# An eight-expert layer's lists in a four-layer transformer: the work beside the pieces goes three steps at a time, the next block's gathers are issued sooner, a layer norm's product changes its engine, and masked keys are made a cycle ahead

## The chip, the cores and the metric

The kernel is one launch on one core of one Trainium2 chip. The metric is the device time of the launch in microseconds (us), lower is better. A core has five engines that run side by side, each through its own instructions in order: TensorE (PE, matrix products and transposes), VectorE (DVE), ScalarE (ACT), GpSimd (POOL) and SyncE (SP, which here only issues transfers). They wait for one another, and for transfers, by semaphores.

## The reference

Four layers run over 4096 tokens of 128 numbers, 16 sequences of 256. Each layer adds a gated attention and a gated feed-forward part, both behind a layer norm that is scaled and shifted per sequence. Cut to what matters here:

```python
def _layernorm(x, axis=-1, eps=1e-05):
    m = jnp.mean(x, axis=axis, keepdims=True)
    v = jnp.var(x, axis=axis, keepdims=True)
    return (x - m) / jnp.sqrt(v + eps)

# layer l
h = _layernorm(x) * (1 + ca) + sa
x = x + ga * attention(h)
h = _layernorm(x) * (1 + cb) + sb
x = x + gb * ffn(h)

# layer 1's ffn: an encoder block of its own
src = ln(src + attention(src), ln1_g, ln1_b)      # 16 heads of 8
gates = softmax(src @ gW + gb)
top2_scores, top2_idx = top_k(gates, 2)
w = (one_hot(top2_idx, 8) * top2_scores[..., None]).sum(1)
h = relu(einsum('nd,edf->enf', src, W1) + b1)
y = einsum('enf,efd->end', h, W2) + b2
out = ln(src + einsum('ne,end->nd', w, y), ln2_g, ln2_b)
```

So each token goes to the two of eight experts with the largest gates. Layer 2's attention has again 16 heads of 8, with rotary positions and a causal mask.

## The kernel before, in words

Activations stand in SBUF with the 128 features on partitions, in eight blocks of 512 tokens. The parts around the change follow one another in time like this.

**Attention in units** (`attend8`). Layer 1's feed-forward part begins with an attention, and layer 2 has one; both go through the same loop. A block holds two sequences, and each is a unit of eight cycles. In a cycle TensorE multiplies keys by queries twice: for the maxima of one unit (`ps_max`, from the masked keys `km` and `q`), reduced on VectorE (`m`, L1342), and for the exponentials of the unit before (`ps_exp`), taken on ScalarE (`E`, L1347). In layer 2 GpSimd masks `E` (L1350). `start_unit` makes a unit's `km` on GpSimd, two products (L1223); it stands at the top of the unit's first cycle. `prepare` makes a block's normed input and its queries and keys, in layer 2 with rotary sums on GpSimd (`q`, L1654); `finish` takes the result on. After each cycle, `advance` lets every generator in `self.later` go one step to its next `yield`. A generator is a piece of work beside: its steps are written out between the cycles of the loop, and so get their places in each engine's order.

**The norm** (`normed_steps`). The mean comes from a product on TensorE, the difference `ln_xc` from VectorE, square, logarithm and exponential (`ln_sq`) from ScalarE, and the last product `xc * sq` from GpSimd.

**The lists.** Beside layer 1's second attention, `gates` routes each block and `listed` writes its tokens into lists by expert in DRAM (`rows`), eight scatters a block from GpSimd (L818); there are two halves of four blocks, with lists of their own. Then the loop over 46 *pieces* of 256 listed rows follows, 23 to a half. A piece's rows and its expert's weights are read by SP (`fetch`), the rows are transposed on TensorE and copied by VectorE (`turn`, `l_x`), two layers of the expert follow (`hidden`, `out`), and ScalarE copies the result and writes it to DRAM (`done`). Reads are two pieces ahead, and one `advance` follows each piece. The half 2 lists of blocks 4 to 7 are still being written when the loop begins.

**The tails.** For each block `tail` gathers the 2 x 512 results from `done`, eight gathers from GpSimd (L1469), two in a step; waits four steps; sums the results with their weights on VectorE (`list_sums`); appends the next block's tail to `later`; and ends with a norm and an addition to `x` on GpSimd. `tail(0)` is appended when half 1's pieces are done. Two buffers of `list_rows` alternate between blocks, and `list_sums` has two as well. What the loop over pieces leaves goes on beside layer 2's attention, whose `prepare` for block b runs `advance` until b + 1 tails are done.

Where `self.strict` is set, instructions stay on their engine in the order of the program text; elsewhere, a scheduler places them. A program order that a line of the text changes is so an order of each engine.

Of the kernel before, what the change touches and what calls it, by code (L numbers as in the profile page):

```python
# [209 lines left out]
def bc(ap, shape):  # L210
    return ap.to_broadcast(shape)


class _InOrder:


    def __init__(self, kernel, engine):
        self.kernel, self.engine = kernel, engine
# [13 lines left out]
class _Kernel:  # L232
    def __init__(self, ctx, tc, t, out):
        self.ctx, self.tc, self.nc, self.t, self.out = ctx, tc, tc.nc, t, out
        self.turn = 0
        self.strict = self.strict_all = False
        self.later = []
        self.in_pieces, self.listed_halves, self.tailed, self.holds = False, 0, 0, {}
        self.tails_begun = self.halves_done = 0
        self.dve, self.act, self.gps = (_InOrder(self, e) for e in (tc.nc.vector, tc.nc.scalar, tc.nc.gpsimd))  # L240


# [120 lines left out]
    def normed_steps(self, src, out):  # L363

        n = src.shape[-1]
        ps = self.bank()[:, :n]
        self.mm(ps, self.c("mean"), src)
        xc = self.ln.tile([P, BLK], F32, tag="ln_xc", name="ln_xc")[:, :n]
        self.dve.tensor_sub(xc, src, ps)
        sq = self.ln.tile([P, BLK], F32, tag="ln_sq", name="ln_sq")[:, :n]  # L370
        self.act.activation(sq, xc, AF.Square)
        yield
        yield
        ps = self.bank()[:, :n]
        self.mm(ps, self.c("mean"), sq)
        self.act.activation(sq, ps, AF.Ln, bias=self.eps5)
        self.act.activation(sq, sq, AF.Exp, scale=-0.5)
        yield
        self.gps.tensor_mul(xc, xc, sq)
        out.append(xc)  # L380
        yield
        yield
# [793 lines left out]
    def attend8(self, nt, group, prepare, finish, scale, causal=False, masks=(None, None)):  # L1176
# [16 lines left out]
        per = len(first)  # L1193
        units = group * NBLK
# [5 lines left out]
        def step(g):  # L1200
            try:
                next(g)
                return True
            except StopIteration:
                return False

        def run(g):
            while step(g):
                pass
# [4 lines left out]
        def start_unit(u):  # L1214
            blk, i = divmod(u, group)
            if i == 0:
                run(ready.pop(blk))
                if blk + 1 < NBLK:
                    ready[blk + 1] = prepared(blk + 1)
            d = U[u]  # L1220
            km = d["km"] = self.att.tile([P, 2, 2, NQ], F32, tag="km", name="km")
            for i in range(2):
                nc.gpsimd.tensor_scalar(km[:, :, i, :], d["k"], half[:, i : i + 1], 0.0, ALU.mult, ALU.add)  # L1223
# [77 lines left out]
        for cycle in range(-lead, units * per):  # L1301
            mx, ex = cycle + lead, cycle
            mu, mt = divmod(mx, per)
            eu, et = divmod(ex, per)
            live_m, live_e = mu < units, ex >= 0
            if live_m and mt == 0:
                start_unit(mu)
            mms = []
            if live_m:
                cs, t, j0 = first[mt]  # L1310
                nk = (t + 1) * P if causal else NQ
                d = U[mu]
                Sm = self.ps_max.tile([P, 1024], F32, tag="max", name="ps_max").rearrange("p (j c i k) -> p j c i k", j=2, c=len(cs), i=2)
                if qmask is not None:
                    for j in range(2):
                        o = Sm[:, j, :, :, nk - P : nk].rearrange("p c i k -> p (c i) k")
                        self.mm(o, self.ident16, bc(qmask.unsqueeze(1), [P, 2 * len(cs), P]), skip_group_check=True)
                for c in range(len(cs)):
                    for j in range(2):
                        r = slice(32 * (j0 + j), 32 * (j0 + j) + 32)  # L1320
                        mms.append((c, Sm[:, j, c, :, :nk], d["q"][r, cs[c], t * P : (t + 1) * P], d["km"][r, cs[c], :, :nk], qmask is None and c == 0))
            if live_e:
                xcs, xt, xj0 = then[et]
                q0 = xt * P if causal else 0
                e = U[eu]
                Se = self.ps_exp.tile([P, 1024], F32, tag="exp", name="ps_exp").rearrange("p (j c i q) -> p j c i q", j=2, c=len(xcs), i=2)
                if kmask is not None:
                    for j in range(2):
                        o = Se[:, j].rearrange("p c i q -> p (c i) q")
                        self.mm(o, self.ident16, bc(kmask.unsqueeze(1), [P, 2 * len(xcs), P]), skip_group_check=True)  # L1330
                for c in range(len(xcs)):
                    for j in range(2):
                        r = slice(32 * (xj0 + j), 32 * (xj0 + j) + 32)
                        mms.append((c, Se[:, j, c, :, q0:], e["k"][r, xcs[c], xt * P : (xt + 1) * P], e["qm"][r, xcs[c], :, q0:], kmask is None and c == 0))
            for c, o, lhsT, rhs, fresh in sorted(mms, key=lambda x: x[0]):
                self.mm(o, lhsT, rhs, start=fresh, skip_group_check=True)
            if live_m:

                a = self.m8[mu % 2][:, t, 8:9]
                dims = [list(a.ap[0]), [32, 2], [2 * P, len(cs)], [P + 16, 2]]  # L1340
                o = bass.AP(tensor=a.tensor, offset=a.offset + 2 * P * cs[0] + 32 * j0, ap=dims)
                nc.vector.tensor_reduce(o, Sm[:, :, :, :, :nk], AX.X, ALU.max, negate=True)  # L1342
            if live_e:
                if xj0 == 0:
                    e["E"] = self.att.tile([P, 4, len(xcs), 2, NQ], F32, tag="E8", name="E8", bufs=3)
                E = e["E"][:, xj0 : xj0 + 2, :, :, q0:]
                nc.scalar.activation(E, Se[:, :, :, :, q0:], AF.Exp, scale=scale)  # L1347
                if causal:
                    D = e["E"][:, xj0 : xj0 + 2, :, :, q0 : q0 + P].rearrange("p j c i q -> p (j c i) q")
                    nc.gpsimd.affine_select(D, D, [[0, 4], [1, P]], ALU.is_ge, 0.0, base=0, channel_multiplier=-1)  # L1350
            for f in held:
                f()
            held = []
            if live_m and mt == per - 1:
                held.append(lambda u=mu: less_maxima(u))
            if live_e and et == 0:
                held.append(lambda u=eu: values(u))
            if live_e and xj0 == 2:
                held.append(lambda u=eu, x=et, E=e["E"]: weighted(u, x, E))
            sides = [g for g in sides if step(g)]  # L1360
            self.advance()
            for g in ready.values():
                step(g)
        for f in held:
            f()
        for g in sides:
# [6 lines left out]
    def layer1_ffn(self):  # L1373
# [12 lines left out]
        nc.vector.tensor_scalar(gg, m[:, 5, :], self.v("i1_ln2_g"), None, ALU.mult)  # L1386
        nc.vector.tensor_scalar(go, m[:, 5, :], self.v("i1_ln2_b"), None, ALU.mult)
        self.list_tables(keep)
        comb = self.comb1
        sums = self.w.tile([P, 4, BLK], F32, tag="m3", name="list_sums")  # L1390
        got = sums[:, 2:, :].rearrange("p a (b j d) -> p (a b) j d", j=2, d=P)
# [2 lines left out]
        with ExitStack() as ctx:  # L1394
# [65 lines left out]
            def tail(blk):  # L1460

                half, t0 = divmod(4 * blk, 16)
                w = self.two_w[half]
                g = self.list_rows[:, 2 * (blk % 2) : 2 * (blk % 2) + 2, :].rearrange("p a (u i d) -> p (a u) i d", i=2, d=P)
                wT, acc = self.h1[:8, :], sums[:, blk % 2, :]
                for t in range(4):
# [1 line left out]
                        of = bass.IndirectOffsetOnAxis(ap=self.origin[half][:, i, t0 + t : t0 + t + 1], axis=0)  # L1468
                        nc.gpsimd.indirect_dma_start(g[:, t, i], None, self.done[half][:, :], of)  # L1469
                    yield  # L1470
                for _ in range(4):
                    yield
                ps = self.bank()
                for t in range(4):
# [6 lines left out]
                for i in range(2):  # L1481
# [3 lines left out]
                            acc[:, v], g[:, t, i], w[:, i, t0 + t : t0 + t + 1], acc[:, v] if i else ps[:, v], ALU.mult, ALU.add  # L1485
                        )
                    yield

                self.tails_begun = blk + 1
                if blk + 1 < 4 * self.halves_done:  # L1490
                    self.later.append(tail(blk + 1))
                y = self.sums_turned(acc)
                yield True
                xb = xf[:, blk * BLK : (blk + 1) * BLK]
# [66 lines left out]
            for n in range(-2, N + 2):  # L1561
                if n + 2 < N:
                    fetch(n + 2)
                if 0 <= n < N:
                    turn(n)
                if 0 <= n - 1 < N:
                    hidden(n - 1)
                if n >= 2:
                    out(n - 2)
                if n == NPIECE + 1:  # L1570
                    self.halves_done = 1
                    self.later.append(tail(0))
                self.advance()
            self.settle()
            self.halves_done = 2
            if self.tails_begun == 4:
                self.later.append(tail(4))
# [20 lines left out]
    def layer2_attn(self):  # L1598
# [5 lines left out]
        with ExitStack() as ctx:  # L1604
# [26 lines left out]
                yield  # L1631

            self.attend8(2, 2, prepare, finish, 1.0 / 11.3125, True, (below, None))

    def turned8(self, w, hb, out):

# [483 lines left out]
```

## Time and profile before

| | |
|---|---|
| time, median of three runs | 3413.59 us (3412.11, 3413.59, 3422.58) |
| the profiled execution | 3419.26 us, of which the span below is 3417.6 |
| PE busy | 3065.4 us, 90% |
| DVE busy | 1961.0 us, 57% |
| ACT busy | 1741.0 us, 51% |
| POOL busy | 1319.5 us, 39% |
| layer 1's second attention | 1770 to 2262 us |
| pieces of half 1, hole, pieces of half 2 | 2262 to 2316, to 2342.5, to 2398.7 us |
| layer 2's attention, up to its first maxima | 2398.7 to 2421.5 us |
| its units 0 to 7, and 8 to 15 | to 2694.8, to 2921 us |

A profile's times are microseconds from the span's start. "Busy" is the time in which an engine ran instructions. A row of the page names line, engine, operation, the tile written and those read, the number of instructions, busy time, mean duration in ns, and idle time of the engine before them with what ended it. L224 is the line of a helper through which VectorE, ScalarE and GpSimd operations go, L266 that of matrix products and L269 that of transposes, so rows are told apart by their tiles. PEclk is the clock that TensorE was granted, as a share of full speed.

### The profile page before, as it was taken

The numbers are of one execution on the slowest core, as the hardware profiler recorded it, in microseconds if no ns is written. First come the engines' busy times: TensorE is split into PE (matmuls) and PEld (weight loads), VectorE is DVE, ScalarE is ACT, GpSimd is POOL, SyncE is SP. The second block draws the span as 40 slices with busy tenths as digits, with TensorE's granted clock in tenths as the row PEclk, the third lists the DMA queues.
The fourth block names the chain that finished last, engine by engine and source line by source line (L and its number), as shares of the span: only waits on it lengthen the run. The fifth ranks groups of instructions, "written<-read, shape, count | busy, mean of one in ns | idle before, by whom it ended". The sixth has DMA issues, their size and how long they took to land. (4 is left out here: it accounts for less than half of the span.)

```text
span 3417.6 us, 51618 instructions
## 1 busy us (share of the span) xinstructions
PE 3065.4 (90%) x19100; PEld 1802.8 (53%) x19100; DVE 1961.0 (57%) x4563; ACT 1741.0 (51%) x4474; POOL 1319.5 (39%) x1167
## 2 busy tenths in 40 slices
PE   6999999979999999999987888886778899899887
PEld 3666666655666677766752333356334444455443
DVE  4777777744444566666654655531345575545564
ACT  3777777754222566666643544444124334575543
POOL 4777777730000233443430122124444343233355
PEclk9999999999999999999987999988789899999998
DMA  3030000000000600000000000036000000000000
GB/s 126 15 37 1 1 1 1 1 25 1 1 1 1 236 1 1 1 1 1 1 1 1 1 12 8 26 117 193 19 13 7 19 1 1 1 1 1 1 13 13
DMA packets 43179, 77.13 MB, mean 23 GB/s; under 512 B 5920, under 2 KB 22736, under 8 KB 42288
## 3 DMA queue, kind: packets, MB, share of 16 engines
q1 hardware_dynamic: 31888, 58.48, 5.8%
q0 software_dynamic: 4416, 9.33, 0.9%
q10 hardware_dynamic: 6624, 6.03, 0.5%
q8 instruction: 151, 2.47, 0.3%
q14 instruction: 100, 0.82, 0.1%
HBM read 44.69 MB, written 33.32 MB: 23 GB/s over the span
## 5 line engine op out<-in xcount | busy, mean ns | idle before, releaser
L224 POOL TENSOR_TENSOR E<-E,sm_inv 128x1024 f32<-128x1024 f32 (+1 forms) x256 | 430.1, 1680 | 480.6 <-PE ps_big L266 189.2
L1342 DVE TENSOR_REDUCE m<-ps_max 128x4 f32<-128x1024 f32 (+1 forms) x256 | 279.3, 1091 | 269.6 <-PE ps_exp L266 178.2
L1347 ACT ACTIVATE E<-ps_exp 128x1024 f32<-128x1024 f32 (+1 forms) x256 | 234.4, 915 | 370.0 <-PE ps_exp L266 289.6
L266 PE MATMUL ps_big<-h,w_f_W 128*128 128x512 f32 x768 | 361.1, 606 | 3.9 <-DVE s L981 3.9
L266 PE MATMUL ps_max<-km,q 32*128 32x512 f32 (+1 forms) x1024 | 296.9, 659 | 74.1 <-DVE m L1342 52.4
L224 ACT ACTIVATE E<-E,sm_neg 128x256 f32<-128x256 f32 x512 | 254.2, 497 | 198.6 <-DVE sm_neg L1071 198.6
L266 PE MATMUL ps_exp<-qm,q 32*128 32x512 f32 (+1 forms) x1024 | 287.6, 640 | 4.4 <-ACT E L1347 4.0
L269 PEld LDWEIGHTS ps_one<-w_cst,E 128*128 128x128 f32 x1792 | 203.6, 141 | 162.6 <-POOL E L224 109.6
L269 PE MATMUL ps_one<-w_cst,E 128*128 128x128 f32 x1792 | 243.3, 276 | 38.6 <-POOL E L224 38.4
L224 DVE COPY PT<-ps_one 128x512 f32<-128x512 f32 x320 | 208.8, 686 | 102.5 <-PE ps_one L269 101.6
L266 PE MATMUL ps_big<-kT,qT 64*128 64x256 f32 (+1 forms) x2048 | 264.9, 377 | 0.0
L266 PEld LDWEIGHTS ps_out<-w_f_W,s 128*128 128x128 f32 (+1 forms) x2048 | 188.6, 190 | 91.3 <-issue 40.4
L266 PE MATMUL ps_one<-PT,v 128*64 128x256 f32 (+1 forms) x2048 | 226.4, 364 | 1.4 <-DVE PT L224 1.0
L224 ACT ACTIVATE E<-ps_big,sm_neg 128x128 f32<-128x128 f32 (+1 forms) x512 | 208.8, 422 | 23.8 <-DVE sm_inv L224 22.0
L1071 DVE CUSTOM_DVE_ANT_0 E<-ps_big,bias 128x256 f32<-128x256 f32 x512 | 186.7, 421 | 48.6 <-PE ps_big L266 37.6
L266 PEld LDWEIGHTS ps_big<-h,w_f_W 128*128 128x128 f32 x768 | 137.7, 191 | 142.2 <-issue 119.9
L224 POOL TENSOR_TENSOR ln_xc<-ln_xc,ln_sq 128x512 f32<-128x512 f32 (+1 forms) x81 | 101.8, 1257 | 283.7 <-ACT ln_sq L224 228.3
L224 POOL TENSOR_TENSOR r_r<-r_r,r_t 128x512 f32<-128x512 f32 x128 | 162.5, 1270 | 124.9 <-DVE r_t L224 112.6
L266 PE MATMUL ps_out<-w_f_W,s 128*128 128x128 f32 (+1 forms) x2048 | 201.0, 281 | 10.4 <-DVE s L1744 10.1
L980 ACT ACTIVATE s<-ps_big,w_vecs 128x512 f32<-128x512 f32 x128 | 87.7, 687 | 222.6 <-PE ps_big L266 222.5
L266 PEld LDWEIGHTS ps_big<-kT,qT 64*128 64x128 f32 x2048 | 166.4, 187 | 58.1 <-issue 49.5
L981 DVE SCALAR_TENSOR_TENSOR s<-ps_big,w_vecs,s 128x512 f32<-128x512 f32 x128 | 95.9, 750 | 167.5 <-ACT s L980 167.5
(318 smaller groups left out, 6092.1 us busy)
## 6 DMA issues: line engine op xcount, KB each, us to landing
rows<-zeros SPq DMA_DIRECT2D x8, 2048.0 KB, 18.5
list_w<-in_f_W SPq DMA_DIRECT2D x46, 257.0 KB, 3.4
list_sums<-rows SPq DMA_DIRECT2D x46, 128.0 KB, 3.2
done<-l_o ACTq DMA_DIRECT2D x46, 128.0 KB, 3.4
rb_rows<-rb_d SPq DMA_DIRECT2D x1, 4088.0 KB
w_a_qkv<-in_a_qkv SPq DMA_DIRECT2D x2, 1536.0 KB
w_f_W<-in_f_W SPq DMA_DIRECT2D x3, 1024.0 KB
bias<-rb_rows SPq DMA_DIRECT2D x16, 192.0 KB, 4.3
```

The source lines that it names most:

```text
L224: ins = f(*args, **kw)
L266: self.ordered(self.nc.tensor.matmul(out, lhsT, rhs, start=start, stop=stop, **kw))
L269: self.ordered(self.nc.tensor.transpose(out, in_, self.c("ident")))
L980: nc.scalar.activation(s, gv[:, :BLK], AF.Silu, bias=self.v("b1_0", c))
L981: nc.vector.scalar_tensor_tensor(s, gv[:, BLK:], self.v("b2_0", c), s, ALU.add, ALU.mult)
L1071: nc.vector.tensor_tensor_reduce(e[:, i], S[:, i], bias[g][:, i, off : off + T], 1.0, BIG, ALU.add, ALU.min, neg[:, i : i + 1])
L1342: nc.vector.tensor_reduce(o, Sm[:, :, :, :, :nk], AX.X, ALU.max, negate=True)
L1347: nc.scalar.activation(E, Se[:, :, :, :, q0:], AF.Exp, scale=scale)
```

## The change

Four edits. The last product of a norm goes to VectorE while `lists_on` is set, which is from the start of layer 1's feed-forward part to the end of layer 2's attention. `start_unit` goes from the top of a unit's first cycle to the end of the cycle before. A tail appends its successor as soon as its own gathers are issued, waits until the tail two before it has summed (its buffer is then free), and between gathers and sums waits nine steps in the loop over pieces, four elsewhere. The loop over pieces calls `advance` three times after each piece.

```diff
     def normed_steps(self, src, out):
...
         yield
-        self.gps.tensor_mul(xc, xc, sq)
+        (self.dve if self.lists_on else self.gps).tensor_mul(xc, xc, sq)
         out.append(xc)
...
             live_m, live_e = mu < units, ex >= 0
-            if live_m and mt == 0:
-                start_unit(mu)
+            if mx == 0:
+                start_unit(0)
             mms = []
...
             for g in ready.values():
                 step(g)
+
+            if live_m and mt == per - 1 and mu + 1 < units:
+                start_unit(mu + 1)
...
         self.list_tables(keep)
+        self.lists_on = True
...
             def tail(blk):

                 half, t0 = divmod(4 * blk, 16)
+                while self.summed < blk - 1:
+                    yield
...
                         nc.gpsimd.indirect_dma_start(g[:, t, i], None, self.done[half][:, :], of)
                     yield
-                for _ in range(4):
+
+                self.tails_begun = blk + 1
+                if blk + 1 < 4 * self.halves_done:
+                    self.later.append(tail(blk + 1))
+                for _ in range(9 if self.in_pieces else 4):
                     yield
...
                     yield
-
-                self.tails_begun = blk + 1
-                if blk + 1 < 4 * self.halves_done:
-                    self.later.append(tail(blk + 1))
+                self.summed = blk + 1
                 y = self.sums_turned(acc)
...
-                self.advance()
+                for _ in range(3):
+                    self.advance()
             self.settle()
+            self.in_pieces = False
             self.halves_done = 2
...
             self.attend8(2, 2, prepare, finish, 1.0 / 11.3125, True, (below, None))
+        self.lists_on = False
```

More of the change, by code (lines that the diff above doesn't have):

```diff
@@ L238, in __init__ @@
         self.in_pieces, self.listed_halves, self.tailed, self.holds = False, 0, 0, {}
-        self.tails_begun = self.halves_done = 0
+        self.tails_begun = self.halves_done = self.summed = 0
+        self.lists_on = False
         self.dve, self.act, self.gps = (_InOrder(self, e) for e in (tc.nc.vector, tc.nc.scalar, tc.nc.gpsimd))
@@ L1633, in layer2_attn @@
             self.attend8(2, 2, prepare, finish, 1.0 / 11.3125, True, (below, None))
+        self.lists_on = False
     def turned8(self, w, hb, out):
```

## The prediction

> **What bounds the kernel now.** I read the page's slices first (a slice is 85 us; digits are tenths busy):
>
> ```profile
> PE   6999999979999999999987888886778899899887
> ...
> DVE  4777777744444566666654655531345575545564
> ...
> POOL 4777777730000233443430122124444343233355
> PEclk9999999999999999999987999988789899999998
> DMA  3030000000000600000000000036000000000000
> ```
>
> TensorE is at 9 tenths except around slices 21 to 31, which hold layer 1's second attention, its lists and layer 2's attention, the stretch that the change touches. The answer by windows splits it:
>
> ```profile
> core 0: us, PE busy (x) PEld busy (x) DVE busy (x) ACT busy (x) POOL busy (x), PEclk, DMA share, GB/s
> ...
> 1770.00:2262.00 492.00, 404.89 (x2694) 161.25 (x2692) 245.90 (x413) 215.18 (x302) 87.04 (x102) 0.88 0.03 10
> 2262.00:2316.00 54.00, 51.23 (x338) 47.93 (x338) 20.76 (x80) 27.28 (x68) 18.21 (x27) 0.92 0.69 206
> 2316.00:2342.50 26.50, 0.03 (x1) 0.06 (x1) 0.00 (x0) 0.22 (x1) 8.70 (x9) 0.54 0.12 37
> 2342.50:2398.70 56.20, 55.90 (x379) 51.16 (x379) 16.36 (x44) 31.77 (x77) 29.00 (x30) 0.97 0.82 244
> 2398.70:2421.50 22.80, 12.79 (x28) 4.25 (x27) 7.07 (x11) 3.60 (x5) 12.84 (x14) 0.83 0.09 26
> 2421.50:2694.80 273.30, 230.03 (x1412) 102.33 (x1416) 142.66 (x245) 83.90 (x135) 119.81 (x138) 0.83 0.05 14
> ```
>
> In order: second attention; pieces of half 1 (one piece is a transpose, two layers of an expert and a write, 1.98 us on PE); a hole of 26.5 us in which only POOL works; pieces of half 2, PE full; layer 2's start; its first four blocks. The chain of waits through the middle:
>
> ```profile
> 2333.04 2.23 DMA rows<-list_rows,l_i
> ...
> 2340.31 2.02 DMA list_sums<-rows
> 2343.13 1.71 PE ps_hid L266 x4
> ...
> 2399.15 1.74 DMA done<-l_o
> ...
> 2405.33 1.27 POOL ln_xc L224
> ...
> 2417.70 1.27 POOL q L1654
> ...
> 2420.47 1.02 PE ps_max L266 x4
> ```
>
> The hole is the list's scatters, each waiting for the one before, 2.50 us apart when quiet. Then PE sets the end up to 2398.7; then latency does, until the first scores. Finally, the lines of the gathers (the 32 before 2420) and of the norm's tile in the second attention:
>
> ```profile
> L1469 POOL DMA_INDIRECT list_rows<-done,origin x32: 947/952/1002, 2351.7 to 2403.0; - x32
> ...
> DMA to landing us min/median/max: 2.5/4.1/4.8
> ```
>
> ```profile
> L224 POOL TENSOR_TENSOR ln_xc<-ln_xc,ln_sq x16: 1255/1270/1282, 1779.2 to 2260.2; 128x512 f32<-128x512 f32 x16
> ...
> L224 DVE TENSOR_TENSOR ln_xc<-x,ps_one x8: 686/687/690, 1775.1 to 2111.7; 128x512 f32<-128x512 f32 x8
> ```
>
> A gather holds POOL 0.95 us; back to back, starts are 1.256 us apart. Under the pieces' DMA load they land after 3.3 to 4.8 us, else after 2.5.
>
> **What the Trainium skill says.** "VectorE: DVE Perf Modes", section on the TRN2 errata: an fp32 tensor_tensor takes (N+151)/0.96, 691 ns at N=512; the 687 above agrees. "GPSIMD Engine Reference", 3.1: the same work is 1.96 times slower there; here 1270/687 = 1.85. "DMA: Bandwidth & Descriptors", Anatomy of one DMA, SWDGE path: about 2.0 us and bytes/436e3, so 2.15 for 64 KB; measured 2.5 quiet, almost twice that loaded. "TensorE: Matmul & The Clock Gate", What's actually happening: an idle window of 3.4 us halves the clock; the 0.54 in the hole agrees.
>
> **The change part by part.** The built programs, compared engine by engine, give the orders below; the number of gathers (64), scatters (64) and pieces (46) is unchanged.
>
> *Masked keys.* No instruction changes place on any engine: end of one cycle and top of the next adjoin. 0.
>
> *Norm's product.* 39 products go from POOL to DVE, 0.58 us shorter each. DVE is half busy there, so they hide; uncovered they would cost 39 x 0.69 = 27 us. In the second attention four products stand behind scatters, which makes DVE wait 2.6 to 3.6 us before them; on DVE their consumers come 1.9 to 2.9 us sooner. Sum 10 us; the other twelve give 0.2 to 0.5 each or the reverse, since max-reduces queue behind them. Between 2 and 10, I take **-6**. In layer 2 22 products shorten by 0.6 a chain of which a part sets the end: 2 to 8, I take **-5**. A POOL stall moves rather than ends: the keys' products (km, L1223) still stand behind eight scatters twice (5 us each).
>
> *Three steps per piece, half 1.* The scatters remain 64, in one chain; neither SP's order of issues nor their number changes. PE waits for the last of half 2 as before; VectorE's wait for block 5's scatters grows from 5 to about 10 us inside the hole. 0 to -2, I take **-0.6**.
>
> *Half 2.* Now tails 0 to 3 are gathered and summed in it (before: all of tail 0, part of 1), and their DVE sums stand at fixed places among the copies x24 to x46 that feed the pieces: tail 0's behind x29, tail 1's x31, tail 2's x35, tail 3's x36. The first gather still waits for the last `done` write of half 1, 2351.7. 32 back to back: the last issues at 2351.7 + 31 x 1.256 = 2390.6 and lands 3 to 4.5 us later, 2393.6 to 2395. Before, x37 was ready near 2372. Behind x36, DVE waits for that landing; nine pieces queue behind x37: 2395 + 9 x 1.98 + about 3 us of tails' PE work = 2416 against 2394.6: **+21.5**. Bounds: +12 if the gathers land early and PE catches up, +25 if the load stretches their 1.256. What is late next is the whole of layer 2.
>
> *Layer 2's start.* Sixteen gathers (tails 4 and 5) now stand on POOL ahead of layer 2's first four q sums (L1654) and four km, and they wait for the last `done` of half 2, 2.8 us after the last piece. 16 x 1.256 = 20.1 us: the q sums begin 23 us after the last piece instead of 12.4, first scores at about 31 instead of 22.8: **+8** (+3 if the gathers begin before the last write lands, +11).
>
> *Layer 2's first eight units.* Before, tails 1 to 7 were done in them, with one hole of 14.1 us in unit 0 for tail 1, and gathers in bursts of eight, in which km or the causal mask's select (E, L1350) came 1.4 to 6.1 us late. Now tails 4 to 7 fall in units 0 to 3, and units 4 to 7 have none. Blocks without tails took 54.1, 56.1 and 50.5 us for two units. Units 4 to 7: 124.8 to 107, -18. Units 0 to 3, 148.3: the hole less 2, so -12, and three forced tails fewer against four bunched tails, -3. Sum **-33**, bounds -20 (bunched gathers hold the selects) and -50 (units 0 to 3 near 54 per block, and the clock, 0.50 there in the first 40 us, higher).
>
> Sum: -6 - 0.6 + 21.5 + 8 - 33 - 5 = -15 us. The profiled execution had a span of 3417.6 us and took 3419.3; the median of the runs is 3413.6, 5.7 lower. 3413.6 - 15 = about **3399 us**.
>
> **Rivals.**
>
> *POOL's queue becomes the bound (slower).* Place: from the first gather of half 2 to unit 3. The +29.5 of pieces and start is paid in full; then the last eleven gathers and tails 6 and 7 stand among the selects of units 0 to 3, so these give nothing, and the units give only -18; products give -1 instead of -11. +29.5 - 18 - 1 = +10.5, 3424. With the products at -1 the kernel is slower once units 0 to 7 take more than 245 us, by over 0.3% above 255. For it: POOL's share there is 44%, and its gathers held selects before. Against: fewer tails are left.
>
> *Even.* Half 2 and start at +30, units at -25, products at -5: 0, 3410 to 3415. For it: both sides are sums of waits that I sized to a third.
>
> *More gain.* Half 2 at +14, start +5, units -50, products -9: -40, 3374. For it: PE is idle 43 us in those units and its clock is 0.83 against 0.94 later, so what removes holes also restores clock. Against: the loss comes first and is near certain.
>
> *The change does nothing.* True of the masked keys, excluded for the rest, whose instructions move on PE, DVE, ACT and POOL.
>
> **How the numbers follow.** What a measurement here can tell from no change is 0.3%, 10.2 us. Chances: my sum, -10 to -30, 0.40; more gain 0.20; even, -10 to +10, 0.25; slower 0.15. So faster 0.60, same 0.25, slower 0.15. Of the rival with more gain I include half and of the slower nearly all: 3374 to 3426. The likeliest case alone is 3384 to 3404.
>
> **What would show it.** Right: unchanged orders' chain to 2342; TensorE waiting inside half 2 between 2365 and 2395, its releaser a copy x behind list_sums; the last piece near 2410; 16 gathers in a row ahead of the first q; first max-reduce near 2445; units 0 to 7 in 235 to 245 us with the 14 us hole gone; no gathers after unit 3. Wrong: no hole inside half 2, so that the sums wait for nothing (then a gain of 30 or more); units 4 to 7 still at 30 us each (then clock, not tails, set them, and the result is even or slower); a second attention longer than 492 us, with DVE's products in front of its max-reduces.

## The result, and the profile after

The changed kernel took 3406.09 us at the median of 15 runs (3398.76 to 3416.51), the kernel before 3415.35 in the same comparison (3406.17 to 3429.49). The ratio is 0.9965, 95% interval 0.9951 to 0.9979: 0.35% faster, which is the 12 us between the two means; the medians differ by 9.3. The forecast was 3399 us and -15.

The profiled execution of the changed kernel happens to be the slowest of its fifteen, at the lowest clock (0.946, up to 0.952 in the others): it took 10.4 us more than its median, the profiled execution of the kernel before 3.9 more. So the two profiles differ by 2.8 us only, and stages are read one by one. The slices of the page after:

```profile
PE   5999999979999999999987888886789989899887
...
DVE  4777777744444566666654656532356675545564
...
POOL 4777777730000233443430021124343333234355
PEclk9999999999999999999997999977789999999998
DMA  3030000000000600000000000044200000000000
```

The DMA's two full slices (3 and 6) have become 4, 4 and 2: the pieces' transfers are spread over a longer time. GpSimd's busy time fell by 48 us to 1271.3, VectorE's rose by 23 to 1984.0. By windows, with the same columns as before (busy us and instructions of the engines, clock, DMA share, GB/s):

```profile
core 0: us, PE busy (x) PEld busy (x) DVE busy (x) ACT busy (x) POOL busy (x), PEclk, DMA share, GB/s
1770.00:2257.70 487.70, 398.43 (x2709) 160.64 (x2705) 256.58 (x432) 215.44 (x302) 67.61 (x90) 0.89 0.04 11
2257.70:2312.40 54.70, 50.67 (x329) 47.33 (x329) 18.41 (x76) 27.24 (x68) 16.40 (x23) 0.88 0.68 203
2312.40:2339.00 26.60, 0.00 (x0) 0.00 (x0) 0.00 (x0) 0.35 (x1) 8.66 (x9) 0.56 0.11 33
2339.00:2419.50 80.50, 72.21 (x423) 60.62 (x424) 29.43 (x75) 38.31 (x89) 36.08 (x36) 0.89 0.62 176
2419.50:2451.70 32.20, 14.28 (x27) 4.67 (x25) 7.83 (x12) 3.59 (x5) 22.95 (x24) 0.69 0.15 41
2451.70:2690.20 238.50, 208.78 (x1356) 92.74 (x1356) 138.76 (x230) 76.07 (x123) 86.46 (x107) 0.87 0.04 12
```

The hole is as long as before. Half 2 went from 56.2 to 80.5 us, layer 2's start from 22.8 to 32.2, its first eight units from 273.3 to 238.5. Measured between marks that both traces share (the first maxima of an attention or a unit on VectorE, the first and last copies of rows in a half), and put beside the forecast:

| stage | before | after | difference | forecast |
|---|---|---|---|---|
| second attention, to the first piece's copy | 473.7 | 469.1 | -4.5 | -6 |
| half 1 and the hole | 77.9 | 78.8 | +0.9 | -0.6 |
| half 2, first copy to last | 51.5 | 75.3 | +23.8 | +21.5 |
| last copy to layer 2's first maxima | 26.9 | 36.7 | +9.8 | +8 |
| units 0 to 7 | 273.3 | 238.4 | -34.8 | -33, and most of -5 |
| units 8 to 15 | 200.7 | 200.7 | 0.0 | the rest of -5 |
| what follows | 518.8 | 520.6 | +1.8 | 0 |

The rows add up to -3 us, as the profiles do. The three stages of the lists (half 2, start, units 0 to 7) come to -1.2 together, the attention to -4.5. Where the rest of the 12 us lies, no stage of these two executions shows.

The start is seen in the chain of waits after. 16 gathers stand on GpSimd ahead of the first q sum; these are the last of them:

```profile
2427.64 6.71 PE ps_one L267 x10
2434.38 0.70 DVE q L1664
2435.32 0.96 POOL list_rows L1476
...
2441.61 0.95 POOL list_rows L1476
2442.58 1.28 POOL q L1665
2443.89 0.76 DVE rot_t L1662
...
2449.07 1.37 POOL km L1224 x2
2450.48 1.22 PE ps_max L267 x4
```

VectorE has its part of q ready at 2435; the sum begins at 2442.58. In half 2, VectorE's waits after are these:

```profile
engine line waited for: us in total, times, longest us
...
DVE list_sums L224 <- PE ps_one L267: 6.8, 4, 3.9
DVE list_sums L224 <- DMA list_rows<-done,origin: 5.3, 5, 1.6
DVE ln_xc L224 <- POOL x L224: 4.0, 1, 4.0
```

Only 5.3 us are waits for a gather to land, which the prediction made the cause of half 2's growth, and all of them fall into the sums of tails 0 and 1, before 2372. The times agree all the same: the 32nd gather was issued at 2389.3 and landed at 2393.0, copy x37 followed at 2394.7 and x46 at 2415.0. Between copies x36 (2387.3) and x37 VectorE ran tail 2's difference, tail 3's sums and the copy; the brackets hold its idle time before each, and what ended it:

```profile
2391.64 0.69 DVE L224 TENSOR_TENSOR ln_xc<-list_sums,ps_one 128x512 f32<-128x512 f32 x1 [3.97 <-POOL x L224]
2392.66 1.12 DVE L224 SCALAR_TENSOR_TENSOR list_sums<-list_rows,list_room,ps_one 128x128 f32<-128x128 f32 x4 [0.33 <-PE ps_one L267]
...
2394.75 0.42 DVE L1540 COPY l_x<-ps_in 128x256 f32<-128x256 f32 x1
```

It waited 4.0 us for GpSimd's addition of tail 0, which stands behind all 32 gathers, and for no gather. TensorE's waits in half 2, apart from the one that ends the hole:

```profile
PE ps_one L270 <- DVE list_sums L224: 6.0, 4, 2.4
PE ps_one L267 <- ACT h L224: 1.0, 1, 1.0
```

### The profile page after: what moved, and what is told of

Same layout as the page of the kernel before. It is cut to its first block, busy times and chain, and to the rows that moved or that the text cites. A ratio compares the mean times of both kernels' runs of the same rounds, so it can differ in the third digit from the quotient of the medians.

```text
span 3414.8 us, 51574 instructions
## 1 busy us (share of the span) xinstructions
PE 3058.7 (90%) x19100; PEld 1804.4 (53%) x19100; DVE 1984.0 (58%) x4602; ACT 1740.6 (51%) x4474; POOL 1271.3 (37%) x1128
## 4 chain that ended last, share of the span: by engine, by line
PE 61%; DVE 10%; ACT 4%; POOL 4%; DMA 3%; issue 3%; POOLq 0%; DVEq 0%; SPq 0%; ACTq 0%
PE ps_one L267 21%; PE ps_big L267 14%; PE ps_out L267 9%; PE ps_max L267 7%; PE ps_one L270 7%; DVE m L1343 4%; DMA rows<-list_rows,l_i 2%; PE ps_exp L267 2%; POOL E L224 1%; ACT ln_sq L224 1%; DVE ln_xc L224 1%; PE ps_hid L267 1%; DVE pv L224 1%; ACT E L1348 1%; POOL list_rows L1476 1%
## 5 line engine op out<-in xcount | busy, mean ns | idle before, releaser
L267 PE MATMUL ps_max<-km,q 32*128 32x512 f32 (+1 forms) x1024 | 289.1, 643 | 79.6 <-DVE m L1343 59.0
L267 PE MATMUL ps_exp<-qm,q 32*128 32x512 f32 (+1 forms) x1024 | 280.2, 625 | 4.4 <-ACT E L1348 4.0
L224 ACT ACTIVATE E<-ps_big,sm_neg 128x128 f32<-128x128 f32 (+1 forms) x512 | 208.8, 422 | 23.8 <-DVE sm_inv L224 21.8
L267 PEld LDWEIGHTS ps_max<-km,q 32*128 32x128 f32 x1024 | 84.0, 199 | 199.4 <-DVE m L1343 98.9
```

The costliest lines, as they stand in the source:

```text
L224: ins = f(*args, **kw)
L267: self.ordered(self.nc.tensor.matmul(out, lhsT, rhs, start=start, stop=stop, **kw))
```

## The experiments

These runs come from three chips: e1 to e4 from one, e5 to e8 from a second, e9 to e12 from a third. On them the kernel before took 3451 to 3457 us at the median instead of 3415, so they are compared with each other only, by ratios to the kernel before beside them on the same chip. Stage times of different chips are compared with some care: e4 and e6, one kernel on two of them, agree within 3 us in each stage. Stage times (us) are from one profile each, between the marks of the table above; "e" numbers are the order of the runs.

| kernel | attention | half 2 | start | units 0-7 | units 8-15 | ratio to before, 95% |
|---|---|---|---|---|---|---|
| e1 masked keys alone | 481.2 | 77.2 | 33.3 | 274.6 | 200.8 | 1.0002 (0.9984 to 1.0020) |
| e2 norm alone | 466.1 | 77.4 | 32.9 | 259.9 | 194.0 | 0.9914 (0.9886 to 0.9942) |
| e3 all but the norm | 483.4 | 97.9 | 36.2 | 238.5 | 201.7 | 0.9987 (0.9967 to 1.0006) |
| e5 the changed kernel | 465.8 | 98.4 | 36.6 | 237.3 | 200.7 | 0.9936 (0.9912 to 0.9961) |
| e4, e6 sums later | 466.5, 469.1 | 81.3, 81.5 | 27.1, 27.2 | 236.5, 236.5 | 194.7, 194.2 | 0.9872 (0.9843 to 0.9902), 0.9845 (0.9820 to 0.9870) |
| e7 gathers in text order | 466.0 | 98.1 | 28.6 | 232.0 | 200.7 | 0.9885 (0.9859 to 0.9910) |
| e8 one step per piece | 463.2 | 77.7 | 34.0 | 257.2 | 197.9 | 0.9910 (0.9885 to 0.9936) |
| e9 no tail in half 2 | 466.5 | 45.8 | 71.9 | 259.2 | 194.8 | 0.9939 (0.9915 to 0.9963) |
| e10 addition on VectorE | 466.3 | 97.0 | 36.7 | 237.0 | 200.7 | 0.9938 (0.9918 to 0.9958) |
| e11 norm and three steps | 466.3 | 108.2 | 36.7 | 234.3 | 200.5 | 0.9949 (0.9931 to 0.9966) |
| e12 e6 and e7 together | 469.5 | 82.9 | 26.6 | 234.5 | 200.7 | 0.9836 (0.9809 to 0.9862) |

### Masked keys alone (e1)

```diff
-            if live_m and mt == 0:
-                start_unit(mu)
+            if mx == 0:
+                start_unit(0)
...
+            if live_m and mt == per - 1 and mu + 1 < units:
+                start_unit(mu + 1)
```

> The kernel before with the masked keys' edit alone. My theory: no engine's order changes, so the time is that of before, ratio 1.000 within 0.2%, and every stage of the profile stands within 1 us of before's where the clock is the same. Rival: making km earlier removes its waits; then the units of both attentions would shorten by 3 us or more in all.

The ratio is 1.0002: this edit does nothing that shows within 0.2%. Its stages serve as those of the kernel before from here on. They were not within 1 us of the profile that was predicted from, which I had expected of them: half 2 took 77.2 us instead of 51.5, with the same instructions. That is taken up under e9.

### The norm's product, alone and left out (e2, e3)

```diff
-        self.gps.tensor_mul(xc, xc, sq)
+        (self.dve if self.lists_on else self.gps).tensor_mul(xc, xc, sq)
```

> The kernel before with the norm's product on VectorE alone. My theory: -6 us between the first and last max-reduce of layer 1's second attention (422.9 to 417), pieces and hole unchanged, and -5 in layer 2's first eight units (273.3 to 268): ratio 0.997. Rival 1, the lists carry the whole gain: 0 to -2, ratio 1.000. Rival 2, the norm is the whole gain and the lists' edits are worth nothing net: ratio 0.9965, units near 265.

> The changed kernel with the norm's product back on GpSimd. My theory: the second attention as before (423 us); pieces of half 2 longer than the changed kernel's 75 us from first to last copy of rows, since the tails' products then queue behind 32 gathers and VectorE's copies behind them: 80 to 90; start +9, units near 240: ratio 1.000 to 1.004. Rival, the lists carry the gain by themselves: half 2 as in the changed kernel or shorter, ratio 0.998 or less.

Norm alone gave 0.86%, far more than forecast: -15.1 us in the attention, -14.7 in units 0 to 7, -6.8 in the units after. The other edits alone gave 0.13%, within their interval of nothing. In the changed kernel the norm's worth is e3 to e5: -17.6 us in the attention, -1.2 in units 0 to 7, -1.0 after. So in units 0 to 7 the product and the lists' edits take away the same time, and only one of them is paid. (The -6.8 after them can't be put down to the product: see e12.)

That is rival 2 of e2, in sense if not in number: beside the norm, the lists' edits were worth nothing. Half 2, start and units 0 to 7 take 370.2 us together with the norm alone, 372.3 in the changed kernel (e5), and the ratios are 0.9914 and 0.9936. Half 2 did not suffer from products on GpSimd (97.9 against 98.4): I had expected 80 to 90 against 75, 5 to 15 more.

Why the attention is shorter was a surprise too. First the windows over it of e1, then of the changed kernel e5:

```profile
1790.50:2271.60 481.10, 398.39 (x2678) 160.22 (x2678) 247.15 (x411) 210.12 (x294) 81.77 (x91) 0.87 0.04 11
```

```profile
1790.70:2256.50 465.80, 382.50 (x2686) 156.70 (x2686) 254.83 (x434) 210.59 (x296) 63.41 (x81) 0.91 0.04 11
```

TensorE's idle time is the window less its busy time: 82.7 us and 83.3. It did not fall. Nearly the same products took 15.9 us less, at a granted clock of 0.91 instead of 0.87. On e1's own chip e2 shows the same: 13.5 us less busy at 0.90, with 81.1 us idle. What TensorE waits for in that window, e1 and then e5:

```profile
PE ps_max L266 <- DVE m L1342: 54.2, 56, 2.7
PE ps_max L266 <- POOL km L1223: 10.8, 2, 5.7
PE ps_one L266 <- DVE a L1283: 4.4, 2, 2.2
```

```profile
PE ps_max L267 <- DVE m L1343: 60.0, 61, 1.7
PE ps_max L267 <- POOL km L1224: 11.0, 2, 6.0
```

The waits of 2.2 and 2.7 us are gone, more short ones have come, and the two on km stay. Of five waits over 2 us two are left, both on km. Fewer long waits and the higher clock go together in every profile here: with the product on GpSimd (the kernel before, e1, e3) the clock of this stage is 0.87 to 0.88, with it on VectorE (all others) 0.89 to 0.91. That the one causes the other is argued, not shown.

### The changed kernel again, and the sums later (e4, e5, e6)

```diff
-                for _ in range(9 if self.in_pieces else 4):
+                for _ in range(30 if self.in_pieces else 4):
                     yield
```

> The changed kernel with a wait of 30 steps instead of 9 between a tail's gathers and its sums in the loop over pieces, so that tails 2 and 3 are summed in layer 2; its built order also has the four q sums and four km ahead of the 16 gathers. My theory, VectorE's in-order waits for the tails hold the pieces' copies: half 2 falls from 75 us to 52 to 56, the start from 32 to 22 to 24, units 0 to 7 rise from 238 to 250 to 256 for two more tails; ratio 0.992 to 0.994. Rival 1, the gathers' transfers themselves or the tails' work on TensorE slow the pieces: half 2 stays over 65. Rival 2, what leaves half 2 comes back in full in the units: 265 and over, ratio 0.9965 as the changed kernel.

> The changed kernel again, beside the next three on one chip. The runs so far were on a chip where the kernel before needs 67 us instead of 43 from the first gather to the last copy of rows. My theory: the change costs some 22 us in half 2 and 8 to 10 in the start wherever it runs, and gives back 33 to 38 in units 0 to 7: ratio 0.995 to 0.999. Rival: on such a chip half 2 waits for transfers already, so that the tails' sums are hidden there and half 2 costs less than 15: ratio below 0.994.

> The wait of 30 steps again, now on the same chip as the changed kernel. My theory: against the changed kernel half 2 is shorter by 15 to 22 us, the start by 8 to 10, and units 0 to 7 stand within 5 us of it, as two more tails in them cost nothing that shows: 20 to 30 us faster than the changed kernel in all. Rival: half 2 is shorter by under 8 us, and what is faster is the start alone.

Against e1, the changed kernel has +21.2 us in half 2, +3.3 from the last copy to the first maxima (+7.0 from the last piece's end, as e1's last piece takes 3.7 us longer), and -37.3 in units 0 to 7: what the change costs and gives in half 2 and in the units is nearly the same as in the first comparison (+23.8, -34.8). With the attention's -15 the ratio is 0.9936 here. That is better than the 0.995 to 0.999 I had expected and is the rival's number, but not for the rival's reason, since half 2 costs as much as before.

With tails 2 and 3 out of half 2 (e6), that stage fell by 16.9 us, the start by 9.4, and the units did not grow, where I had expected 250 to 256 us for e4. Half 2 stayed over 65, as rival 1 of e4 had it. e6 stands at 0.9845 and e5 at 0.9936 of the same kernel before: faster than both, and than the change by 0.9%, 34 us at the medians. Windows over half 2, start and units, e5 and then e6:

```profile
2334.10:2432.50 98.40, 74.44 (x390) 60.64 (x390) 28.39 (x75) 35.47 (x82) 35.75 (x36) 0.80 0.50 139
2432.50:2469.10 36.60, 20.40 (x59) 9.37 (x57) 8.08 (x14) 6.13 (x12) 22.90 (x24) 0.71 0.15 43
2469.10:2706.40 237.30, 211.03 (x1356) 94.19 (x1356) 139.14 (x230) 75.95 (x123) 86.47 (x106) 0.87 0.04 12
```

```profile
2333.40:2415.00 81.60, 63.62 (x350) 53.87 (x350) 19.03 (x49) 31.03 (x74) 33.75 (x34) 0.81 0.60 167
2415.00:2442.20 27.20, 18.18 (x68) 9.33 (x67) 8.17 (x14) 6.72 (x13) 7.25 (x8) 0.87 0.06 20
2442.20:2678.70 236.50, 212.10 (x1388) 95.53 (x1386) 148.59 (x256) 80.18 (x130) 105.01 (x125) 0.91 0.06 16
```

The size fits my theory, but this run doesn't single out VectorE's waits: it takes away two tails' products on TensorE as well. TensorE's busy time fell by 10.8 us, its idle time by 6.0 (24.0 to 18.0). Rival 1's second half, the tails' work on TensorE, therefore holds for the larger part. In the units, 32 more products fitted into the same time: idle time fell from 26.3 to 24.4, and the clock rose to 0.91.

### The gathers in the order of the text (e7)

```diff
-                        nc.gpsimd.indirect_dma_start(g[:, t, i], None, self.done[half][:, :], of)
+                        ins = nc.gpsimd.indirect_dma_start(g[:, t, i], None, self.done[half][:, :], of)
+                        if not self.in_pieces:
+                            self.tc.keep_in_program_order(ins)
```

> The changed kernel with each gather that is written after the loop over pieces kept behind what stands before it on GpSimd in the program text: the 16 gathers then follow the four q sums and the first unit's km. My theory: the start falls by 8 to 10 us, half 2 as in the changed kernel, units 0 to 7 longer by 0 to 5, since the second unit's km and later selects wait for gathers: 4 to 9 us faster than the changed kernel. Rival: the time goes into unit 0, which waits for the km behind 16 gathers: same as the changed kernel.

The start fell by 8.0 us, half 2 stayed, and the units fell by 5.3 instead of rising: unit 1 took 31.0 us instead of 38.6. That is over my 4 to 9 us; the ratios differ by 0.5%, some 18 us, of which 13 are in these stages. The 16 gathers ahead of q cost what the prediction said, and where they stand now units 0 to 3 did not grow for them (129.2 us, 134.3 in e5).

### Which of the lists' edits shortens the units (e8, e11)

```diff
-                for _ in range(3):
-                    self.advance()
+                self.advance()
```

> The changed kernel with one step beside per piece instead of three; the tails' gathers still begin sooner and the norm is on VectorE. Tails 0 and 1 are summed among the pieces, 2 to 7 in layer 2. My theory, that the three steps are what puts the tails' chains in front of the pieces' copies: half 2 within 5 us of the kernel before, start 22 to 24, and units near 240, since what shortens them is the gathers' early start and not where the sums are: 20 us faster than the changed kernel. Rival, the three steps are what gives the gain in the units: units 255 to 265, and as fast as the norm alone.

In e8, by the program's text, tails 2 and 3 meet in the buffer of turned gates, so that part of the bias sums of one block is formed with another block's gates. The kinds, sizes and numbers of instructions are not touched by this. The other half (e11) is the kernel with the three steps and the norm, but each tail begun when the one before has summed. Against the kernel before, the norm and masked keys left out:

```diff
+                for _ in range(3):
+                    self.advance()
-                self.advance()
...
                     yield

                 self.tails_begun = blk + 1
                 if blk + 1 < 4 * self.halves_done:
                     self.later.append(tail(blk + 1))
                 y = self.sums_turned(acc)
```

> The kernel before with the norm on VectorE and three steps per piece, but each tail still begun only when the one before it has summed. Theory A, that the units' gain needs the tails to overlap: units 0 to 7 near 255 to 260 as with the norm alone, or as with one step and early gathers (257). Theory B, that the three steps bring it by having tails done before layer 2: 236 to 245. Half 2: between the norm alone (77) and the changed kernel (98), as three to four tails are summed in it.

One step per piece leaves half 2 as in e1 (77.7), which fits my theory, but the units at 257.2 and the ratio of the norm alone, which is the rival's. Three steps without early gathers bring the units to 234.3. So the three steps give the units' gain, as theory B says, and early gathers are worth the difference of e11 and e5: half 2 shorter by 9.8 us, units longer by 3.0 (e10, on e11's chip, stands as e5 does). My view that early gathers shorten the units fell. Theory B's reason, more tails done before layer 2, is not shown either. e6 and e8 both have six tails' sums in the units; in e6 they lie in units 0 to 3 and cost nothing, in e8 in units 0 to 5, and the units take 20.7 us longer. What decides this wasn't isolated.

### No tail in half 2 (e9)

```diff
-                if n == NPIECE + 1:
-                    self.halves_done = 1
-                    self.later.append(tail(0))
...
+                if n == 2 * NPIECE - 1:
+                    z = keep.tile([P, 1], F32, tag="last", name="last")
+                    self.mark = nc.gpsimd.tensor_copy(z, o[:, 0, :1])
...
+                        with self.tc.issue_after(self.mark.ins):
+                            nc.gpsimd.indirect_dma_start(g[:, t, i], None, self.done[half][:, :], of)
...
-            if self.tails_begun == 4:
-                self.later.append(tail(4))
+            self.later.append(tail(0))
```

> The changed kernel with no tail begun before the last piece: a one-column copy on GpSimd reads that piece's result, and all gathers are issued behind it. Question: on this chip the kernel before already needs 77 us from the first copy of half 2 to the last, against 51.5 in the profile that was predicted from. If the gathers' transfers take the DMA engines from the pieces' reads: 23 pieces at 2 us, 46 to 52 here too. Rival, the pieces' own reads and writes are slower on this chip: 60 or more. In either case the start grows by some 40 us, as 30 gathers and a whole tail stand before layer 2, so this kernel is not meant to be faster.

Windows over half 2, of e1 and then of e9:

```profile
2349.60:2426.80 77.20, 60.36 (x345) 52.40 (x345) 14.27 (x38) 29.20 (x71) 25.90 (x27) 0.81 0.62 172
```

```profile
2329.30:2375.10 45.80, 45.80 (x310) 43.10 (x310) 9.36 (x23) 26.52 (x66) 0.00 (x0) 0.95 0.85 252
```

45.8 us, TensorE never idle, 252 GB/s against 172. The pieces' own transfers are not slow; it is the tails begun among them that cost half 2 of e1 31 us, in which TensorE is idle for 16.8 and does 35 more products at a lower clock. In the first comparison (51.5) the same tails cost about 6 by this measure. e9 and e1 ran on different chips, but not so that e9's would explain it: e10, beside e9, took 97.0 us where e5 took 98.4.

The traces show where the time goes. Here are 10 us of half 2 in which GpSimd begins eight gathers one behind the other, first in the first comparison's kernel before and then in e1:

```profile
2370.00:2380.00 10.00, 10.00 (x69) 8.98 (x68) 3.71 (x9) 5.69 (x15) 7.56 (x9) 1.00 0.94 268
```

```profile
2370.00:2380.00 10.00, 1.82 (x10) 1.35 (x10) 0.00 (x0) 0.84 (x2) 7.56 (x9) 0.59 0.21 56
```

In the first, the pieces' reads and writes go on beside the gathers, at 268 GB/s in all. In the second hardly anything but the gathers moves, at 56 GB/s, and TensorE, VectorE and ScalarE all but stand still until the 16th gather is issued at 2380.2. Of the 16.8 us that TensorE is idle in e1's half 2, 16.0 lie in stretches with gathers, and e5 has one of 20 us at 52 GB/s. Why this happens in these runs and not in the first comparison stays open; the launches differ in it, not the program.

### Tail 0's addition on VectorE (e10)

```diff
-                self.gps.tensor_add(xb, xb, n)
+                (self.dve if self.in_pieces else self.gps).tensor_add(xb, xb, n)
```

> The changed kernel with the tails' last addition to x on VectorE while the pieces run. In the changed kernel's profile tail 2's difference waits 4 us on VectorE for tail 0's addition, which stands on GpSimd behind all 32 gathers and holds one of two ln_xc buffers. My theory, that this wait and the landing of tail 3's last gather end together: half 2 shorter by 0 to 3 us against the changed kernel's 98.4. Rival, GpSimd's queue and not the landing is what sets it: shorter by 4 to 8.

Half 2 went from 98.4 to 97.0, and the ratio stayed (0.9938 and 0.9936): within my 0 to 3 us. But the run tests less than it was made for. The 4 us wait on GpSimd's addition, plain in VectorE's waits of the first comparison, isn't among those of e5, so there was no such wait to take away. For the first comparison its trace gives a bound: the last gather landed 1.7 us before copy x37, so without the wait x37 could have come at most that much sooner.

### Both together (e12)

The edits of e6 and e7 stand in one kernel.

> The wait of 30 steps together with the gathers after the loop kept in the order of the program text. Both shortened something of their own: the first took tails 2 and 3 out of half 2, the second took unit 1 from 38 to 31 us. If the second's gain stands beside the first: units near 231, ratio to before 0.983 or less. Rival: the wait of 30 steps already leaves GpSimd's queue in that order, so nothing is left: 0.9845 to 0.987.

0.9836 against 0.9845, intervals 0.005 wide: not to be told apart. Units 0 to 7 gained 2 us of the 5 hoped for, and units 8 to 15 took 200.7 us again where e6 took 194.2. Units 8 to 15 show one of two lengths, near 194 (e2, e4, e6, e9) or near 200.7 (e1, e3, e5, e7, e10, e11, e12), with or without the norm on VectorE; e8 lies between. What decides it wasn't found.

## Why the prediction was right, and where it was not

The sum was -15 us; the ratio says -12 (-7 to -17); the sign and the range held. Part of that is luck: the lists' edits, which were to bring -3.5 net (+21.5, +8, -33), brought about nothing beside the norm in the experiments, while the norm, which was to bring -11, carried the gain.

- **Masked keys, 0.** Right (e1).
- **Norm in the attention, -6 from shorter waits behind scatters.** The profile shows -4.5, the experiments -15 to -18. The mechanism failed: TensorE's idle time stayed and its clock rose. In the first comparison too: 79.3 us idle before and 82.0 after, 7.2 us less busy. "Two to ten" was too narrow, since it priced waits alone.
- **Norm in layer 2, -5.** Too small for the edit alone (-14.7 in units 0 to 7 in e2); wrong inside this change, where e3 and e5 differ by -2.2. I added two edits' gains that remove the same waits.
- **Half 1, -0.6.** +0.9; the chain of scatters set it, as said.
- **Half 2, +21.5 by the landing of the last gather.** The size was right (+23.8 and +21.2), the path was not, so that the times agreed is in part luck. Behind x36, VectorE waited for GpSimd's addition and not for the landing. TensorE, which was to wait between 2365 and 2395 for a copy of rows behind the sums, waited 2.5 us there and 8.3 in all, never for a copy. The end did follow x37 as written: nine pieces and "about 3 us of tails' PE work", which measures 3.7. What the sum has no term for is the tails' work on TensorE ahead of x37; it took that to be hidden under the wait. TensorE's groups in half 2 (PE, columns as in the page's part 5), before and then after, show it:

```profile
L266 PE MATMUL ps_one<-w_f_b,h 8*128 8x128 f32 x16 | 2.3, 283 | 0.0
L269 PE MATMUL ps_one<-w_cst,list_sums 128*128 128x128 f32 x8 | 1.2, 273 | 0.0
L269 PE MATMUL ps_one<-w_cst,list_room 128*8 128x128 f32 x8 | 1.2, 272 | 0.0
L266 PE MATMUL ps_one<-list_sums,w_cst 128*128 128x512 f32 x2 | 1.0, 594 | 0.0
L266 PE MATMUL ps_one<-ln_sq,w_cst 128*128 128x512 f32 x2 | 1.0, 594 | 0.0
```

```profile
L267 PE MATMUL ps_one<-w_f_b,h 8*128 8x128 f32 x32 | 4.6, 283 | 1.0 <-ACT h L224 1.0
L267 PE MATMUL ps_one<-list_sums,w_cst 128*128 128x512 f32 x8 | 4.3, 619 | 0.9 <-DVE list_sums L224 0.9
L267 PE MATMUL ps_one<-ln_sq,w_cst 128*128 128x512 f32 x8 | 4.2, 606 | 0.4 <-ACT ln_sq L224 0.4
L270 PE MATMUL ps_one<-w_cst,list_sums 128*128 128x128 f32 x16 | 4.1, 344 | 6.0 <-DVE list_sums L224 6.0
L270 PE MATMUL ps_one<-w_cst,list_room 128*8 128x128 f32 x16 | 3.3, 346 | 0.0
```

  6.7 us of tails' products became 20.5: +13.8, all but 3.7 of the 20.5 ahead of x37. From the windows, half 2 is 24.3 us longer, 16.3 of it busy and 8.0 idle. TensorE was full there before, so work moved in could not be free. But that isn't the whole reason: in e1 it was idle for 16.8 of 77.2 us, and the change cost as much there (e5: 14.1 us more busy, 7.1 more idle).
- **Start, +8.** Right, in size (+9.8) and mechanism: putting the gathers behind q took 8.0 us off (e7).
- **Units 0 to 7, -33.** Right in size (-34.8): -21.8 in units 4 to 7 (forecast -18) and -12.9 in units 0 to 3 (-15). No gather came after unit 3, as forecast. But that fewer tails are left is not the reason: e6 has two tails more in them and is as short. What three steps change is seen from e8 to e5: TensorE's idle time falls from 35.5 to 26.3 us, and it does 41 products less in the units, at a clock of 0.87 instead of 0.86. From before to after, idle time fell from 43.3 to 29.7 us, with 56 products less and a clock of 0.87 instead of 0.83; three single waits of 4.7 to 6.1 us on km, an addition to x and a select have become two, of 3.9 and 4.4.
- **The slower rival** needed units above 245 us. They took 238, so it failed at its own mark; its first half, +29.5 from half 2 and the start, came true in full (+33.6).

## What to carry to other kernels

When work beside is moved to an earlier stage, count its time on the engine that bounds that stage, and not only the waits that it brings: here the tails' 13.8 us on TensorE were more than half of what half 2 grew by, and two of the four moved tails were better left in layer 2, where TensorE was idle for a ninth of the time and they cost nothing (e6). Two edits that each shorten the same waits don't add up, so cost the second one in a kernel that has the first, and test each alone: the norm's edit alone was no slower than all four. And read the order of every queue that a moved step issues to: 16 gathers ahead of four small sums cost 8 us, and one line put them behind.

## What the runs showed of the hardware

- TensorE's granted clock carried a gain of 16 us (0.87 to 0.91 over 470 us, e1 and e5) while its idle time stayed at 83 us; of the waits over 2 us, five had become two.
- The kernel before needed 51.5 us for half 2 in one comparison, and e1, the same instructions, 77.2 in another; without gathers among the pieces half 2 took 45.8 (e9).
- In 10 us with eight gathers the DMA engines moved 268 GB/s and TensorE was busy throughout in one launch; in another (e1) they moved 56 GB/s, and TensorE was busy for 1.8 us.
